# Two graph layers on one core: the second feed-forward products by seven instead of eight in one layer, first products planned first, head products one group at a time, and the layer norm's aggregation on GpSimd

## The chip, the core and the metric

The kernel runs on one core of a Trainium2 chip. Its engines work side by side: TensorE (PE in the profile; its weight loads are PEld) multiplies matrices, VectorE (DVE), ScalarE (ACT) and GpSimd (POOL) do element-wise work, and SyncE (SP) issues the transfers between device memory and the core's SBUF. Matmul results land in PSUM, in 8 banks of 128 partitions by 512 f32 numbers. The metric is the device time of one execution in microseconds (us).

## The reference

64 graphs of 256 nodes and 256 features go through two layers; everything is f32. The inputs are `x` (64, 256, 256) and a 0/1 matrix `adj` (64, 256, 256).

Layer 0 applies graph attention twice and a feed-forward:

```python
Wh = h @ W;  e = leaky_relu(Wh @ a[:F] + (Wh @ a[F:]).T, 0.2)
att = softmax(where(adj > 0, e, -9e15), axis=1);  h = att @ Wh          # twice
h = layernorm(x + h);  h = layernorm(h + relu(h @ w_ff1 + b_ff1) @ w_ff2 + b_ff2)
```

Layer 1 is attention with 8 heads of 32 whose weights are not masked before the softmax; afterwards the values of relation r are summed over the entries where `adj == r` (only 0 and 1 occur), and a feed-forward follows:

```python
attn = softmax(q @ k.T / sqrt(32));  out = sum_r (attn * (adj == r)) @ (src @ Wv[r])
x = layernorm(src + out @ Wo);  x = layernorm(x + gelu(x @ W1 + b1) @ W2 + b2)
```

Both feed-forwards are 256 to 1024 to 256.

## The kernel before, in words

**Tiling.** Two graphs form a pair; 32 pairs go one after another through `whole_way`: `gat_layers`, `feed_forward` (stage 0), `attention`, `feed_forward` (stage 2), and the output's transfer. Activations lie as 4 tiles of 128 nodes by 256 features.

**First feed-forward products (line 689) and query, key and value products (764, 769).** They use a scheme with seven products of matrix halves instead of eight (Strassen's, in Winograd's form). Class `Blocks` holds its steps, named by product: `p1`, `p2`, `p6`, `p5`, `p7`, `p4`, `p3`. Each is two matmuls of 256 columns. The sums of the weights are made once, those of the activations in `Second`. Some products add into a bank that still holds a predecessor: `p6` goes into the bank of `p1` once ScalarE has copied that (line 695), and `p7` into the bank of `p6`, again after a copy. A feed-forward has two such sets of slabs, `a` and `b`, interleaved in one list of steps. ScalarE then applies bias and function (line 701), 16 activations per feed-forward.

**Second feed-forward products (line 720).** By the plain way: for each of two groups of rows `b` and halves `j`, eight matmuls of 256 columns are summed in one bank, 32 in all. `add_rows` (571) adds the bank to the rows, and `layernorm` follows: VectorE's statistics and aggregation (581, 582), GpSimd's root in four small operations (587 to 590), ScalarE's normalisation (594).

**Attention.** Four head groups per pair (two graphs by two sets of four heads). `scores` (809) runs four 32-row matmuls side by side, ScalarE takes the exponentials (818), VectorE masks (822) and half-sums (826) them. `products` (840, 843) runs four 32-column matmuls side by side and sums the weights by a matmul with ones; VectorE takes the reciprocal of a whole 128x256 block (852) and multiplies (853); ScalarE checks the range (850). The head products of two groups are planned together.

**What sets the order.** Nothing loops over pairs at run time: a planner, `run`, writes one fixed order per engine while the program is built. Every piece of VectorE, ScalarE, GpSimd and SP work is given to `put` with an assumed duration, a rank and the events that it waits for; TensorE's work is written as generators that `yield` the events and the number of banks that their next step needs. `run` keeps a clock per engine, always takes the engine that can begin first, and on it the piece of lowest rank. On TensorE it picks among up to four pairs, plus `reliefs` (work on the weights at the start):

```python
g = going[min(sure, key=lambda n: (going[n][0] is besides, "ff" in (going[n][2] or ()) or alone.get("ff") is going[n][0], n))
```

So a pair in its feed-forward comes after all pairs that are elsewhere; only one pair at a time may be in a feed-forward (`alone["ff"]`), and one in attention. `hurried` names the stages in which rows are transposed on TensorE (line 655) instead of through device memory.

## Time and profile before

| | |
|---|---|
| median of 3 runs | 3081.23 us (3080.15 to 3081.99) |
| profiled execution, its own time | 3077.64 us |
| its span, first to last instruction | 3075.9 us |
| mean granted TensorE clock | 0.994 |
| TensorE busy | 3010.9 us, 19154 matmul records |
| TensorE weight loads busy | 2454.7 us |
| VectorE busy | 2234.0 us |
| ScalarE busy | 1835.1 us |
| GpSimd busy | 1032.2 us |

An f32 matmul appears as two records, each with its weight load. Records of consecutive matmuls overlap, so their mean duration (380 ns at 256 columns) is longer than the distance from one start to the next. A line number is that of the program text; several layers share a line, and tile names tell them apart (`w_L_gnn_w_ff` is layer 0, `w_L_gnn_W` layer 1).

### The profile page before, as it was taken

To read this page: it belongs to the slowest core of one execution; us is meant where nothing else is said; L and a number is where in the kernel's file an instruction comes from. 1 tells how busy PE (TensorE), PEld (TensorE's weight loads), DVE (VectorE), ACT (ScalarE), POOL (GpSimd) and SP (SyncE) were. 2 spreads that over 40 slices of the span, in tenths; PEclk is the share of its full clock that TensorE was granted. 3 is DMA by queue.
4 is the path that set the end of the run, shared out by engine and by line. 5 is a ranking of instruction groups with operands and counts; after the bars stand their busy time and mean duration, and the time that the engine had idled before them with its cause. 6 is when DMAs were issued, how large, how long until landed. Compare 5 with 4: busy or idle time off the path is not lost.

```text
span 3075.9 us, 52423 instructions
## 1 busy us (share of the span) xinstructions
PE 3010.9 (98%) x19154; PEld 2454.7 (80%) x19154; DVE 2234.0 (73%) x4411; ACT 1835.1 (60%) x4186; POOL 1032.2 (34%) x1542
## 2 busy tenths in 40 slices
PE   7999999999999999999999999999999999999998
PEld 6877778877878788887888778878788778788876
DVE  5787766788776867768677676686776777767774
ACT  4556665656665566565756566565666565655654
POOL 1332244232423243232352322533325333233223
PEclk8999999999999999999999999999999999999999
DMA  6211132102321122211231122311213211121000
GB/s 181 73 51 36 56 124 79 46 28 75 109 66 50 61 76 80 73 49 56 76 99 60 42 70 69 97 66 50 66 54 96 82 53 57 62 93 58 32 1 22
DMA packets 211865, 205.76 MB, mean 67 GB/s; under 512 B 22928, under 2 KB 171280, under 8 KB 211600
## 3 DMA queue, kind: packets, MB, share of 16 engines
q1 hardware_dynamic: 211184, 202.06, 20.5%
q8 instruction: 154, 2.52, 0.3%
q14 instruction: 111, 0.91, 0.1%
q10 hardware_dynamic: 416, 0.26, 0.0%
HBM read 137.51 MB, written 64.73 MB: 66 GB/s over the span
## 4 chain that ended last, share of the span: by engine, by line
PE 79%; DVE 10%; ACT 3%; DMA 3%; POOL 2%; issue 2%; SPq 1%; DVEq 0%; POOLq 0%; ACTq 0%
PE ps L720 24%; PE ps L689 20%; PE ps L840 6%; PE ps L764 6%; PE ps L769 6%; PE ps L809 4%; PE ps L545 3%; PE ps L529 3%; PE ps L862 2%; PE ps L843 2%; DVE e L502 2%; DVE x L571 2%; DVE st L581 1%; PE ps L558 1%; DMA home<-yb 1%
## 5 line engine op out<-in xcount | busy, mean ns | idle before, releaser
L587 POOL TENSOR_SCALAR less<-mv 128x2 f32<-128x2 f32 x256 | 65.4, 255 | 1596.6 <-DVE mv L582 1561.4
L594 ACT ACTIVATE x<-x,less,rstd 128x256 f32<-128x256 f32 x512 | 279.3, 594 | 418.8 <-POOL less L590 414.9
L720 PE MATMUL ps<-w_L_gnn_w_ff,ff 128*128 128x256 f32 x2048 | 466.4, 380 | 0.0
L720 PE MATMUL ps<-w_L_gnn_W,ff 128*128 128x256 f32 x2048 | 461.7, 380 | 0.9 <-ACT ff L701 0.9
L720 PEld LDWEIGHTS ps<-w_L_gnn_W,ff 128*128 128x128 f32 x2048 | 386.9, 190 | 61.0 <-issue 5.4
L720 PEld LDWEIGHTS ps<-w_L_gnn_w_ff,ff 128*128 128x128 f32 x2048 | 387.9, 190 | 57.2 <-issue 4.3
L393 DVE TENSOR_TENSOR ff<-ps,ff 128x512 f32<-128x512 f32 x384 | 261.1, 683 | 163.6 <-PE ps L689 127.1
L822 DVE TENSOR_TENSOR m<-a,adj 128x1024 f32<-128x1024 f32 x256 | 325.4, 1271 | 20.6 <-ACT a L818 20.5
L689 PE MATMUL ps<-yT,w_L_gnn_W1p 128*128 128x256 f32 x1280 | 316.1, 384 | 10.9 <-ACT ff L695 7.4
L689 PE MATMUL ps<-yT,w_L_gnn_w_ff1p 128*128 128x256 f32 x1280 | 312.4, 384 | 12.3 <-ACT ff L695 12.3
L818 ACT ACTIVATE a<-ps 128x512 f32<-128x512 f32 x512 | 266.8, 603 | 68.0 <-PE ps L809 67.1
L689 PEld LDWEIGHTS ps<-yT,w_L_gnn_W1p 128*128 128x128 f32 x1280 | 238.3, 190 | 61.8 <-ACT ff L695 17.9
L689 PEld LDWEIGHTS ps<-yT,w_L_gnn_w_ff1p 128*128 128x128 f32 x1280 | 241.3, 191 | 56.6 <-ACT ff L695 16.7
L571 DVE TENSOR_TENSOR x<-ps,x 128x512 f32<-128x512 f32 x256 | 173.0, 680 | 152.4 <-PE ps L720 120.3
L695 ACT ACTIVATE ff<-ps 128x512 f32<-128x512 f32 x384 | 221.1, 589 | 92.0 <-PE ps L689 90.1
L604 POOL TENSOR_TENSOR x<-x,b_L_gnn_g_ln 128x512 f32<-128x512 f32 x128 | 168.7, 1318 | 274.5 <-DVE yb L623 138.3
L852 DVE RECIPROCAL h<-ps 128x256 f32<-128x256 f32 x128 | 224.1, 1752 | 49.1 <-PE ps L843 48.9
L581 DVE BATCH_NORM_STATS2 st<-x 128x6 f32<-128x256 f32 x512 | 208.4, 407 | 4.7 <-issue 0.4
L701 ACT ACTIVATE ff<-ff,c_L_gnn_b_ff 128x256 f32<-128x256 f32 x384 | 174.4, 509 | 49.4 <-DVE ff L393 48.8
L604 POOL TENSOR_TENSOR x<-x,b_L_gnn_g 128x512 f32<-128x512 f32 x128 | 166.1, 1298 | 94.4 <-ACT x L594 74.8
L589 POOL TENSOR_TENSOR rstd<-rstd,mhalf 128x2 f32<-128x2 f32 x256 | 189.1, 739 | 21.3
L701 ACT ACTIVATE ff<-ff,c_L_gnn_b 128x256 f32<-128x256 f32 x384 | 172.0, 502 | 31.6 <-DVE ff L393 31.0
(138 smaller groups left out, 5499.8 us busy)
## 6 DMA issues: line engine op xcount, KB each, us to landing
home<-yb SPq DMA_DIRECT2D x182, 256.0 KB, 2.0
yT<-home SPq DMA_DIRECT2D x728, 64.0 KB, 2.0
rows<-row SPq DMA_DIRECT2D x60, 512.0 KB, 3.8
input<-in_xT SPq DMA_DIRECT2D x32, 512.0 KB, 4.0
x<-in_x SPq DMA_DIRECT2D x32, 512.0 KB, 4.1
out<-x SPq DMA_DIRECT2D x32, 512.0 KB, 2.9
input<-in_adjT SPq DMA_DIRECT2D x30, 512.0 KB, 4.1
v<-in_adjT SPq DMA_DIRECT2D x2, 512.0 KB, 6.6
```

What stands on the lines that cost most here:

```text
L393: nc.vector.tensor_tensor(self.target(c, h), self.bank[bank], self.target(c, h), ALU.add)
L571: return put("vector", 0.6, lambda: nc.vector.tensor_tensor(rows, p, rows, ALU.add), *events, frees=["bank"])
L581: nc.vector.bn_stats(st[:, j, :], rows[j])
L594: nc.scalar.activation(rows[j], rows[j], AF.Identity, bias=less[:, j:j + 1], scale=rstd[:, j:j + 1])
L604: nc.gpsimd.tensor_tensor(both, both, v.rearrange("p (k d) -> p k d", k=1).to_broadcast([P, 2, D]), op)
L689: nc.tensor.matmul(to, lhsT=w1[:, a, (t + slab) * P:(t + slab + 1) * P], rhs=b, **flags)
L695: return put("scalar", 0.5, lambda: nc.scalar.activation(target(c, h), blocks.bank["x"], AF.Copy), event, rank=-1)
L701: evacuated[h][m] = put("scalar", 0.4, lambda m=m, to=to, source=source: nc.scalar.activation(to, source, func, bias=b1[:, m:m + 1]), even ...
L720: nc.tensor.matmul(p2[:, j * D:(j + 1) * D], lhsT=f[m][:, (2 * j + b) * P:(2 * j + b + 1) * P], rhs=w2[:, m, :], start=m == 0, stop=m == N ...
L818: nc.scalar.activation(a[n][q][:, k], ps[2 * q + k], AF.Exp)
L822: nc.vector.tensor_tensor(m[n][q], a[n][q], adj, ALU.mult)
L852: there = put("vector", 1.68, lambda: nc.vector.reciprocal(s, po[:, N:]), there, rank=0)
```

## The change

- `SEVEN = (0,)`: the second feed-forward products of stage 0 (layer 0) are made by `by_seven`, with seven products of halves of 4 x 2 matmuls of 128 columns each. `last_weights` loads that weight in four parts and `last_sums` makes four differences of them. VectorE makes four combinations of the activations in place (`combine`, 128x1024) and adds the products to the rows as they come (`add`). Stage 2 keeps the plain way (`by_eight`). The activations now lie in four tiles, one for each quarter.
- `degree`: first feed-forward products come before other pairs' work, second ones after it. `filling` marks the pair whose second products are under way. Five pairs may be in flight instead of four.
- Head products are planned for one head group at a time, and the order of a few steps in attention moves.
- The reciprocal works on 8 numbers per partition between two transposes of 32x32 blocks; the range check works on those.
- The layer norm's aggregation of two half-row statistics moves from VectorE to GpSimd, whose root has nine operations.
- `put_each` gives exponentials, normalisations, statistics and scalings to the planner one instruction at a time, ranked by when the first was ready.

```diff
...
+SEVEN = (0,)
...
+    def put_each(engine, us, emits, *events, rank=1, frees=(), needs=None, function=None):
+        before = None
+        for emit in emits[:-1]:
+            before = put(engine, us, emit, *events, rank=rank, lag=0.0, needs=needs, function=function, behind=before)
+            events, needs = [before], None
+        return put(engine, us, emits[-1], *events, rank=rank, frees=frees, function=function, behind=before)
...
+        def degree(g):
+            if g[0] in filling:
+                return 2
+            return 0 if "ff" in (g[2] or ()) or alone.get("ff") is g[0] else 1
...
-                g = going[min(sure, key=lambda n: (going[n][0] is besides, "ff" in (going[n][2] or ()) or alone.get("ff") is going[n][0], n))
+                g = going[min(sure, key=lambda n: (going[n][0] is besides, degree(going[n]), n))
-                piece = waiting[engine].pop(min(able, key=lambda n: (waiting[engine][n]["rank"], waiting[engine][n]["ready"])))
+                piece = waiting[engine].pop(min(able, key=lambda n: (waiting[engine][n]["rank"], waiting[engine][n]["first"]["ready"])))
...
+    def last_weights(name):
+        s = const.tile([P, 7, NF // 2, P], F32, name="w_" + name)
+        for c, h, at in ((1, 0, 0), (0, 0, 1), (0, 1, 2), (1, 1, 3)):
+            nc.sync.dma_start(s[:, at], t[name][c * FF // 2:(c + 1) * FF // 2, h * P:(h + 1) * P].rearrange("(k p) d -> p k d", p=P))
+        return s
+    def last_sums(w, there, event):
+        for to, a, b in ((4, 3, 0), (5, 2, 4), (6, 2, 3), (3, 1, 5)):
+            there = put("vector", 0.6, lambda to=to, a=a, b=b: nc.vector.tensor_tensor(w[:, to], w[:, a], w[:, b], ALU.subtract),
+                        there, rank=5, event=event if to == 3 else None)
...
-        st = mv = rstd = less = None
+        st = rstd = less = None
         rows = [r[:, 2 * b + j, :] for j in range(2)]
-        def statistics():
-            nonlocal st, mv
-            st, mv = small.tile([P, 2, 6], F32, name="st"), small.tile([P, 2, 2], F32, name="mv")
-            for j in range(2):
-                nc.vector.bn_stats(st[:, j, :], rows[j])
-                nc.vector.bn_aggr(mv[:, j, :], st[:, j, :])
+        def statistics(j):
+            nonlocal st
+            if j == 0:
+                st = small.tile([P, 2, 6], F32, name="st")
+            nc.vector.bn_stats(st[:, j, :], rows[j])
         def root():
             nonlocal rstd, less
-            rstd, less = small.tile([P, 2], F32, name="rstd"), small.tile([P, 2], F32, name="less")
-            nc.gpsimd.tensor_scalar(less, mv[:, :, 0], -1.0, None, ALU.mult)
-            nc.gpsimd.tensor_scalar(rstd, mv[:, :, 1], EPS, None, ALU.add)
+            rstd, less, both, apart = (small.tile([P, 2] if n < 2 or n == 3 else [P, 2, 2], F32, name=name)
+                                       for n, name in enumerate(("rstd", "less", "both", "apart")))
+            halves = [st[:, :, 3 * n + 1:3 * n + 3] for n in range(2)]
+            nc.gpsimd.tensor_tensor(apart, halves[0][:, :, 0], halves[1][:, :, 0], ALU.subtract)
+            nc.gpsimd.tensor_tensor(both, *halves, ALU.add)
+            nc.gpsimd.tensor_tensor(apart, apart, apart, ALU.mult)
+            nc.gpsimd.tensor_scalar(rstd, both[:, :, 1], 1.0 / D, EPS, ALU.mult, ALU.add)
+            nc.gpsimd.tensor_scalar(apart, apart, 0.25, None, ALU.mult)
+            nc.gpsimd.tensor_scalar(less, both[:, :, 0], -0.5, None, ALU.mult)
+            nc.gpsimd.tensor_tensor(rstd, rstd, apart, ALU.add)
             nc.gpsimd.tensor_tensor(rstd, rstd, mhalf[:, :2], ALU.pow)
             nc.gpsimd.tensor_tensor(less, less, rstd, ALU.mult)
-        def normalise():
-            for j in range(2):
-                nc.scalar.activation(rows[j], rows[j], AF.Identity, bias=less[:, j:j + 1], scale=rstd[:, j:j + 1])
-        there = put("vector", 0.9, statistics, *events)
-        there = put("gpsimd", 1.5, root, there, rank=0)
-        return put("scalar", 0.8, normalise, there)
+        def normalise(j):
+            nc.scalar.activation(rows[j], rows[j], AF.Identity, bias=less[:, j:j + 1], scale=rstd[:, j:j + 1])
+        there = put_each("vector", 0.35, [lambda j=j: statistics(j) for j in range(2)], *events)
+        there = put("gpsimd", 2.7, root, there, rank=0)
+        return put_each("scalar", 0.5, [lambda j=j: normalise(j) for j in range(2)], there)
...
+        yield from (by_seven if stage in SEVEN else by_eight)(y, normal, f, evacuated, w2, w2_there, b)
+        for g in range(2):
+            normal[g] = layernorm(y, g, *normal["added"][g])
+            if onwards:
+                transposed(y, normal[g], normal, g, pair, 1)
+            else:
+                normal[g] = scaled(y, ln[3], g, normal[g])
+        filling.clear()
+        done_with("ff")
+    def by_eight(y, normal, f, evacuated, w2, w2_there, last):
+        half, order, normal["added"] = NF // 2, (0, 1, 4, 5, 2, 3, 6, 7), []
+        filling.append(alone["ff"])
...
-                        nc.tensor.matmul(p2[:, j * D:(j + 1) * D], lhsT=f[m][:, (2 * j + b) * P:(2 * j + b + 1) * P],
+                        nc.tensor.matmul(p2[:, j * D:(j + 1) * D], lhsT=f[c][j][:, k, g * P:(g + 1) * P],
                                          rhs=w2[:, m, :], start=m == 0, stop=m == NF - 1)
...
+            normal["added"].append([add_rows(y, p2, g, there, normal["scaled", g])])
+    def by_seven(y, normal, f, evacuated, w2, w2_there, last):
...
+        half = NF // 2
+        (a22, a12), (a21, a11) = f
+        def done(j, c):
+            return evacuated[j][c * half:(c + 1) * half]
+        def product(n, to, side, first=False):
+            for b in range(2):
+                for k in range(half):
+                    nc.tensor.matmul(to[:, b], lhsT=side[:, k, b * P:(b + 1) * P], rhs=w2[:, n - 1, k],
+                                     start=first and b == k == 0, stop=True, skip_group_check=True)
+            return took(1.8)
+        def add(to, of, us, *events, frees=()):
+            return put("vector", us, lambda: nc.vector.tensor_tensor(to, of, to, ALU.add), *events,
+                       *(normal["scaled", b] for b in range(2)), rank=-1, frees=frees)
+        def combine(to, a, b, op, *events):
+            return put("vector", 1.14, lambda: nc.vector.tensor_tensor(to, a, b, op), *events, rank=0)
+        def two_halves():
+            return bank().rearrange("p (j b d) -> p j b d", j=2, b=2)
+        rows = y.rearrange("p (b j) d -> p j b d", j=2)
+        def quarter(j, h):
+            return rows[:, 1 - j, :, h * P:(h + 1) * P]
+        yield [w2_there, *done(0, 0)], None, 1
+        left = two_halves()
+        read4 = product(4, left[:, 0], a22, True)
+        t1 = combine(a22, a21, a22, ALU.add, *done(0, 0), *done(0, 1), read4)
+        t3 = combine(a21, a11, a21, ALU.subtract, *done(1, 1), t1)
+        yield done(1, 1), None, 1
+        x = two_halves()[:, 0]
+        read1 = product(1, x, a11, True)
+        d1 = add(quarter(0, 0), x, 0.34, read1)
+        t2 = combine(a11, a22, a11, ALU.subtract, t3, read1)
+        yield from last.p3()
+        frees_at(clock["tensor"], ["yT", "sums_yT"])
+        filling.append(alone["ff"])
+        yield [t1], None, 1
+        v = two_halves()[:, 0]
+        read5 = product(5, v, a22, True)
+        d5 = add(quarter(1, 1), v, 0.34, read5)
+        yield [t2, d1], None, 0
+        d6 = add(quarter(0, 1), x, 0.34, product(6, x, a11))
+        yield done(1, 0), None, 0
+        read2 = product(2, left[:, 1], a12)
+        d24 = add(rows[:, :, :, :P], left, 0.6, read2, read4, frees=["bank"])
+        t4 = combine(a12, a12, a11, ALU.subtract, t2, read2)
+        yield [t3, d6], None, 0
+        d7 = add(rows[:, 0].rearrange("p b (h d) -> p b h d", h=2),
+                 x.rearrange("p b (h d) -> p b h d", h=1).to_broadcast([P, 2, 2, P]), 0.6, product(7, x, a21), d5, frees=["bank"])
+        yield [t4, d5], None, 0
+        d3 = add(quarter(0, 1), v, 0.34, product(3, v, a12), frees=["bank"])
+        normal["added"] = [[d24, d7, d3]] * 2
...
-            def weight(q):
-                a[n][q] = work.tile([P, 2, 512], F32, name="a", bufs=HQ)
-                for k in range(2):
-                    nc.scalar.activation(a[n][q][:, k], ps[2 * q + k], AF.Exp)
+            def weight(q, k):
+                if k == 0:
+                    a[n][q] = work.tile([P, 2, 512], F32, name="a", bufs=HQ)
+                nc.scalar.activation(a[n][q][:, k], ps[2 * q + k], AF.Exp)
...
+            blocks = s.rearrange("p (g i) -> p g i", i=32)
+            both = []
+            def invert():
+                both.append(small.tile([P, 2, N // 32], F32, name="inverse", bufs=4))
+                nc.vector.transpose(s, po[:, N:])
+                nc.vector.tensor_copy(both[0][:, 1], blocks[:, :, 0])
+                nc.vector.reciprocal(both[0][:, 0], both[0][:, 1])
+                nc.vector.transpose(blocks, both[0][:, 0].rearrange("p (g i) -> p g i", i=1).to_broadcast([P, N // 32, 32]))
             def check():
-                for of, c in ((s, 0), (po[:, N:], 1)):
-                    nc.scalar.activation(of, of, AF.Copy, accum_out=reach[:, pair, c, n:n + 1])
-            there = put("vector", 1.68, lambda: nc.vector.reciprocal(s, po[:, N:]), there, rank=0)
-            there = put("vector", 0.34, lambda: nc.vector.tensor_tensor(to, po[:, :N], s, ALU.mult), there, rank=0)
-            put("scalar", 1.0, check, there, frees=["bank", "h"])
-            return there
+                for of in range(2):
+                    nc.scalar.activation(both[0][:, of], both[0][:, of], AF.Copy, accum_out=reach[:, pair, of, n:n + 1])
+            there = put("vector", 1.3, invert, there, rank=0)
+            put("scalar", 0.4, check, there, rank=3)
+            return put("vector", 0.34, lambda: nc.vector.tensor_tensor(to, po[:, :N], s, ALU.mult), there, rank=0, frees=["bank", "h"])
...
-        for step in (a_.p1, b_.p1, a_.p2, a_.p6, b_.p2, a_.p5, b_.p6, a_.p7, b_.p5, a_.p4, b_.p7, lambda: scores(0), a_.p3, b_.p4,  b_.p3, lambda: scores(1)):
+        for step in (a_.p1, b_.p1, a_.p2, a_.p6, b_.p2, a_.p5, b_.p6, a_.p7, b_.p5, a_.p4, b_.p7, a_.p3, b_.p4, lambda: scores(0), b_.p3, lambda: scores(1)):
...
-        for n in (0, 2):
-            yield [*masked[n], *masked[n + 1], ready["v", 0, n // 2], ready["v", 1, n // 2]], None, 2
-            divided += [products(n), products(n + 1)]
-            if n == 0:
-                for later in (2, 3):
-                    yield from scores(later)
+        for n in range(4):
+            yield [*masked[n], ready["v", 0, n // 2], ready["v", 1, n // 2]], None, 1
+            divided.append(products(n))
+            if n < 2:
+                yield from scores(n + 2)
...
-    run(reliefs(), (whole_way(pair) for pair in range(NPAIR)), 4)
+    run(reliefs(), (whole_way(pair) for pair in range(NPAIR)), 5)
...
-    nc = bacc.Bacc("TRN2", target_bir_lowering=False, num_devices=1)
+    nc = bacc.Bacc("TRN2", target_bir_lowering=False, num_devices=1, dynamic_dma_scratch_size=1024)
```

## The prediction

> **What bounds the kernel now.** I read the busy table of the page first, then the groups by shape, TensorE in order of time, the start of the trace, and last TensorE's waits.
>
> ```profile
> PE 3010.9 (98%) x19154; PEld 2454.7 (80%) x19154; DVE 2234.0 (73%) x4411; ACT 1835.1 (60%) x4186; POOL 1032.2 (34%) x1542
> ```
>
> TensorE bounds it. Its busy time hides waits, since overlapping records run 0.38 us each, so I count from start to start.
>
> ```profile
> 1002.24 8.90 PE L720 MATMUL ps<-w_L_gnn_W,ff 128*128 128x256 f32 x40
> 1011.07 1.07 PE L840 MATMUL ps<-a,v 128*32 128x256 f32 x16
> 1011.96 1.05 PE L840 MATMUL ps<-m,v 128*32 128x256 f32 x16
> 1012.82 0.61 PE L843 MATMUL ps<-h,ones 128*32 128x256 f32 x8
> 1013.25 1.05 PE L840 MATMUL ps<-a,v 128*32 128x256 f32 x16
> 1014.12 1.05 PE L840 MATMUL ps<-m,v 128*32 128x256 f32 x16
> 1014.98 0.61 PE L843 MATMUL ps<-h,ones 128*32 128x256 f32 x8
> 1015.53 1.78 PE L862 MATMUL ps<-w_L_gnn_Wo,qk 128*128 128x256 f32 x7
> ```
>
> An f32 matmul leaves two records. Forty records of 256 columns last (8.90 - 0.38)/39 = 0.218 us each, 0.216 in the median: 0.432 us per matmul. The column-tiled head products (L840, L843) stand in blocks of two head groups, 4.46 us for both.
>
> If every record took its own pace (0.216 us at 256 columns, a quarter of that where four run side by side), TensorE would need 2902.6 us. The span is 3075.9: 6.8 us before the first matmul, 12.7 after the last began, and 153.8 beyond the pace. Of these about 54 are entering and leaving the 32-wide blocks (0.31 us for each of 128 score blocks, 0.23 for each of 64 product blocks), 23 are waits of the first 100 us, and 72 are waits between full-width matmuls later.
>
> ```profile
> PE ps L689 <- ACT ff L695: 23.5, 31, 1.7
> PE ps L558 <- ACT xw L510: 11.6, 2, 10.6
> PEld ps L689 <- ACT ff L695: 44.3, 55, 2.1
> ```
>
> Columns: who waited for whom, total us, times, longest. Of the 72 us, 51 are the first feed-forward products (L689) waiting for ScalarE's copy of their own predecessor's bank (L695). Going through the seven-product scheme step by step, 29 of the 51 stand at one step, the seventh product of the second half (p7 of slabs b), and 7 at p6 of slabs a.
>
> [...]
>
> The halved products need 128 columns per freshly loaded weight, which the feed-forward never does here. The start of the trace brackets it:
>
> ```profile
> 51.75 1.86 PEld L933 LDWEIGHTS ps<-c_L_gnn_b_ln2c,wqk 128*128 128x128 f32 x16
> 50.99 1.04 PE L465 MATMUL ps<-ident,rise 128*128 128x128 f32 x8
> 51.86 1.84 PE L933 MATMUL ps<-c_L_gnn_b_ln2c,wqk 128*128 128x1 f32 x16
> ```
>
> Full f32 loads before one-column matmuls: (1.86 - 0.19)/15 = 0.112 us each, which is what the load alone allows[...]. 128-column transposes: (1.04 - 0.27)/7 = 0.109 us, which is what the columns alone allow. At 256 columns the load (0.19 us as recorded) vanishes under the matmul. Overlapped, the pace is the larger, 0.112 us per record, 0.2234 per matmul; in series it would be 0.22 per record. I take 0.112 and keep 0.109 and 0.22 as ends.
>
> **The change, part by part.** Counts are from the two built programs.
>
> *Seven products in the first layer's second half.* 1024 matmuls of 256 columns go (1024 x 0.4317 = 442.1 us), 1792 of 128 come (1792 x 0.2234 = 400.4). On TensorE: **-41.7 us**, all of it on the path. What it adds lies on VectorE: 128 combinations of 128x1024 at L822's mean of 1.27 us (+163) and 128 additions of 256 columns from PSUM at 0.41, the mean of the like-sized L853 (+53); 64 additions of 0.68 replace 64. New waits: product 5 on the first combination, 6 on the third, 3 on the fourth. The built order leaves 4.7 us of other matmuls or more before 5 and 4.4 before 6, but in 14 of 32 stages product 3 follows 2 with only product 7 (1.79 us) between; addition and combination need 0.68 + 1.27 plus handovers, 2.2 or 2.3. 14 x 0.5: **+7 us** (0 if nothing else holds VectorE up and the handovers are short, +25 if its queue adds a microsecond each).
>
> *First products first, second ones last, five pairs at once.* TensorE's work is the same; distances change. p7 of slabs b stands at the bare minimum of two products (1.73 us) behind its predecessor in 53 of 64 feed-forwards before, 17 after; p6 of slabs a in 54 and 64. Scaling the measured losses: 29 x (1 - 17/53) = 20 won, 7 x 10/54 = 1 lost, about **-18 us** after rounding down. From below, nothing is won if ScalarE, which must fit six copies and sixteen activations into one first half, is simply late elsewhere; from above, nearly all 72 go. The end loses cover: before, 24 records and more of another pair's second products stood between the last pair's projections and its feed-forward; after, the last output projection is followed directly by 32 transposes and then the first products. A layer norm costs, by its rows, 0.69 + 0.8 + 2.5 + 1.1 us and handovers, then a copy of 0.6 and one sum of 0.5, minus the transposes: **+8 us**.
>
> *Products per head group.* Runs of head products: 64 before, 120 after, 8 of them still double. A split costs 0.093 (entry) + 0.113 (leaving instead of running on) + 0.025 = 0.231 us: 56 x 0.231 = +12.9. Scores next to products 64 times instead of 8 save an entry of 0.093 each: -5.2. **+7.7 us.** The score-to-product distance shrinks to 6.9-7.2 us at the least (8.3 before); the masks and half sums were done 6.1 to 6.9 us after the scores in the median, up to 10.7, and are needed only 0.9 and 1.8 us into the block. I take no wait; 0.3 us at each would be +35.
>
> *Aggregation on GpSimd.* VectorE loses 512 aggregations (-93 us); GpSimd's root goes from four operations (0.255 + 0.235 + 0.739 + 0.206) to nine, five more at 0.2 or so: +1.06 us x 256 = 271, to 43%. Behind it on GpSimd stand the scalings and shifts (L604), which have 275 us of slack before them. The layer norm becomes 0.7 us longer; other pairs' matmuls hide that except at the two ends.
>
> *Reciprocal by transposes; split ScalarE pieces; table loads.* VectorE: 1.752 us become two transposes of 256 columns (0.44 by interpolation between L475 and L623), a copy and a short reciprocal, 1.25 together: -64. VectorE in sum 2234 + 163 + 53 - 93 - 64 = 2293, 76%. ScalarE: +48 table loads of 1.28 (+62), checks about -50. None on TensorE's path while both stay under 80%; if that cover fails, it shows as waits of L731, priced above.
>
> *Start.* The weights of the second half come by four transfers instead of one and get four sums of 0.69 us, ahead of the second pair's attention weights on VectorE. Two more microseconds of transfers ahead of the bias that TensorE already waits 10.6 us for: **+2**. SP's later issues in the steady state are the same.
>
> Sum: -41.7 + 7 - 18 + 8 + 7.7 + 2 = **-35 us**. Profiled: span 3075.9 to 3041; the profiled execution was 3077.6, 3.6 below the median of 3081.2. Median: **3046 us**.
>
> **Rivals.**
> *The filler works better.* With second products always ready as filler most of the 72 us go, say 60 instead of 18: 3004 us. For it: the ScalarE pieces are finer, and additions rank by the first piece's time. Against: at most one feed-forward runs at a time, so it has no second products to fill its own first half.
> *Gains eaten.* Score-to-product waits and VectorE's longer queue give back 30 us: 3076, no difference. The change then does nothing that can be told (0.2%, 6 us, is about what this kernel's runs resolve).
> *Slower: the narrow products don't reach their pace.* Place: L804. Price: 3584 records, so each nanosecond is 3.6 us. It decides from 35/3584 = 10 ns more, 0.122 us per record; at 0.13 the time is 3111, wholly in series over 3400. For it: load and columns differ by only 3 ns, so any handover shows. Against: loads start 2 ns after the matmul before them in the trace at 256 columns. A VectorE chain late by more than 1.1 us in every pair would end on the same side.
>
> **How the numbers follow.** Forecast 0.60 (its own range 3025 to 3068), better filler 0.14, gains eaten 0.11, slower 0.15. Range 2998 to 3090: it leaves out about 0.05 below and 0.13 above. Faster: 0.60 + 0.14 + a third of the eaten case = 0.78; same 0.07; slower 0.15.
>
> **What would show it.** L804's records 0.112 us apart; TensorE records up by 1536; waits of L731 on L737 near 50 us instead of 68 (both TensorE queues together); head-product runs near 120; an idle TensorE of some 8 us after the last L990; VectorE near 2290, GpSimd near 1300. The prediction is wrong if L804's pace is over 0.12, if waits for VectorE's combinations (L813) exceed 25 us, or if head products (L960) wait for masks.

## The result, and the profile after

The changed kernel takes 3087.67 us (median of 14 runs, 3079.35 to 3095.08) against 3080.14 for the kernel before on the same chips (14 runs, 3075.55 to 3084.40): a ratio of 1.0024, 95% interval 1.0015 to 1.0034. The forecast was 3046 us. The kernel as built became slightly slower, and the forecast had the wrong sign.

The page of the changed kernel, its busy table (engine, busy us, share of the span of 3086.1 us, instructions):

```profile
PE 2986.8 (97%) x20690; PEld 2474.5 (80%) x20690; DVE 2338.3 (76%) x4543; ACT 1831.8 (59%) x4234; POOL 1345.9 (44%) x2822
```

TensorE has 1536 records more, as counted. Its busy share fell from 98% to 97%: it has less to do and waits longer. Its work in order of time (start, duration, line, count), two runs of the narrow products:

```profile
2019.63 3.73 PE L804 MATMUL ps<-w_L_gnn_w_ff,ff 128*128 128x128 f32 x32
2026.20 1.95 PE L804 MATMUL ps<-w_L_gnn_w_ff,ff 128*128 128x128 f32 x16
```

One record lasts 0.277 us in the mean, so the first line gives (3.73 - 0.28)/31 = 0.111 us from start to start, the second (1.95 - 0.28)/15 = 0.111. The pace of 0.112, the forecast's main number, is right, and so is TensorE's gain: summed over all records at their own pace, 2902.5 us became 2860.8, **-41.7 us**. But what TensorE loses beyond that pace rose from 153.8 to 205.6 us. Its waits after the change (who waited for whom, total us, times, longest):

```profile
PE ps L990 <- DVE qk L983: 13.8, 8, 3.3
PE ps L731 <- DVE ff L424: 11.8, 6, 2.8
...
PE ps L731 <- ACT ff L737: 9.2, 10, 1.5
PE ps L804 <- DVE ff L813: 9.0, 6, 2.4
PE ps L701 <- ACT x L640: 7.7, 3, 3.5
...
PE ps L960 <- DVE m L942: 1.8, 2, 1.1
```

Before, the first line was the wait for ScalarE's copies, and the whole of what named VectorE (DVE) was this:

```profile
PE ps L689 <- DVE x L571: 1.0, 1, 1.0
PE ps L689 <- DVE ff L393: 0.7, 1, 0.7
```

Now the first lines are waits for VectorE: adding all lines of this view that name it gives 38.7 us, against 1.7 before. The wait for ScalarE that the forecast wanted smaller did get smaller (23.5 to 9.2).

One such wait can be followed from its cause. VectorE of the changed kernel in order of time; the bracket is idle time before the instruction and what ended it:

```profile
1524.14 0.48 DVE L542 SCALAR_TENSOR_TENSOR e<-rows,ratio 128x256 f32<-128x256 f32 x1 [1.03 <-DMA rows<-row]
1524.66 1.55 DVE L544 SCALAR_TENSOR_TENSOR e<-adj,empty,e 128x256 f32<-128x256 uint8 x1
...
1526.15 1.48 DVE L542 SCALAR_TENSOR_TENSOR e<-rows,ratio 128x256 f32<-128x256 f32 x1
1527.67 1.37 DVE L544 SCALAR_TENSOR_TENSOR e<-adj,empty,e 128x256 f32<-128x256 uint8 x1
...
1528.97 0.68 DVE L424 TENSOR_TENSOR ff<-ps,ff 128x512 f32<-128x512 f32 x1
...
1531.10 0.43 DVE L972 STREAM_TRANSPOSE h<-ps 128x256 f32<-128x256 f32 x1
...
1532.85 1.38 DVE L544 SCALAR_TENSOR_TENSOR e<-adj,empty,e 128x256 f32<-128x256 uint8 x1
...
1534.35 0.40 DVE L983 TENSOR_TENSOR qk<-ps,h 128x256 f32<-128x256 f32 x1
```

GpSimd (POOL) in the same stretch:

```profile
1524.65 1.29 POOL L650 TENSOR_TENSOR x<-x,b_L_gnn_g_ln 128x512 f32<-128x512 f32 x1
1525.89 1.47 POOL L650 TENSOR_TENSOR x<-x,b_L_gnn_g 128x512 f32<-128x512 f32 x1
1527.31 1.44 POOL L650 TENSOR_TENSOR x<-x,b_L_gnn_b_ln 128x512 f32<-128x512 f32 x1
1528.72 1.45 POOL L650 TENSOR_TENSOR x<-x,b_L_gnn_beta 128x512 f32<-128x512 f32 x1
1532.69 1.26 POOL L650 TENSOR_TENSOR x<-x,b_L_gnn_g 128x512 f32<-128x512 f32 x1 [2.52 <-ACT x L640]
```

And TensorE:

```profile
1526.21 0.61 PE L963 MATMUL ps<-h,ones 128*32 128x256 f32 x8
...
1532.10 0.59 PE L990 MATMUL ps<-w_L_gnn_Wo,qk 128*128 128x256 f32 x2
1534.81 1.56 PE L990 MATMUL ps<-w_L_gnn_Wo,qk 128*128 128x256 f32 x6 [2.12 <-DVE qk L983]
```

L542 lasts 0.48 us in the median, L544 0.49. Beside GpSimd's scalings (L650, 1.26 to 1.47 us here) four of them last about as long as one of those: 1.55, 1.48, 1.37 and 1.38. L424, which reads PSUM and SBUF, runs beside L650 in its ordinary 0.68. The head products end at 1526.8; their inversion (the reciprocal by transposes, from L972 on) begins at 1531.1, behind the stretched operations, its multiplication (L983) at 1534.35, behind one more, and TensorE stands still for 2.12 us.

### The profile page after: what moved, and what is told of

The parts are those of the page before. It is cut to its first block, busy times and chain, and to the rows that moved or that the text cites. A ratio compares the mean times of both kernels' runs of the same rounds, so it can differ in the third digit from the quotient of the medians.

```text
span 3086.1 us, 56707 instructions
## 1 busy us (share of the span) xinstructions
PE 2986.8 (97%) x20690; PEld 2474.5 (80%) x20690; DVE 2338.3 (76%) x4543; ACT 1831.8 (59%) x4234; POOL 1345.9 (44%) x2822
## 5 line engine op out<-in xcount | busy, mean ns | idle before, releaser
L629 POOL TENSOR_TENSOR apart<-st 128x2 f32<-128x2 f32 x256 | 55.0, 215 | 1283.4 <-DVE st L622 1281.3
L778 PE MATMUL ps<-w_L_gnn_W,ff 128*128 128x256 f32 x2048 | 475.0, 382 | 3.6 <-ACT ff L743 3.6
L804 PEld LDWEIGHTS ps<-w_L_gnn_w_ff,ff 128*128 128x128 f32 x3584 | 420.2, 192 | 29.0 <-DVE ff L813 12.7
L804 PE MATMUL ps<-w_L_gnn_w_ff,ff 128*128 128x128 f32 x3584 | 429.9, 277 | 10.0 <-DVE ff L813 9.0
L424 DVE TENSOR_TENSOR ff<-ps,ff 128x512 f32<-128x512 f32 x384 | 262.5, 684 | 158.7 <-PE ps L731 97.9
L640 ACT ACTIVATE x<-x,less,rstd 128x256 f32<-128x256 f32 x512 | 285.5, 594 | 115.7 <-POOL less L637 114.5
L942 DVE TENSOR_TENSOR m<-a,adj 128x1024 f32<-128x1024 f32 x256 | 314.0, 1227 | 49.1 <-ACT a L938 49.1
L737 ACT ACTIVATE ff<-ps 128x512 f32<-128x512 f32 x384 | 225.7, 589 | 161.5 <-PE ps L731 159.7
L731 PE MATMUL ps<-yT,w_L_gnn_W1p 128*128 128x256 f32 x1280 | 316.3, 386 | 1.7 <-ACT ff L737 1.0
L731 PE MATMUL ps<-yT,w_L_gnn_w_ff1p 128*128 128x256 f32 x1280 | 307.8, 382 | 0.0
L731 PEld LDWEIGHTS ps<-yT,w_L_gnn_W1p 128*128 128x128 f32 x1280 | 241.5, 192 | 48.1 <-issue 9.5
L731 PEld LDWEIGHTS ps<-yT,w_L_gnn_w_ff1p 128*128 128x128 f32 x1280 | 241.3, 192 | 31.4 <-ACT ff L737 0.2
L650 POOL TENSOR_TENSOR x<-x,b_L_gnn_g 128x512 f32<-128x512 f32 x128 | 181.6, 1421 | 186.9 <-ACT x L640 165.2
L650 POOL TENSOR_TENSOR x<-x,b_L_gnn_g_ln 128x512 f32<-128x512 f32 x128 | 180.9, 1416 | 168.8 <-DVE yb L669 130.4
L551 ACT ACTIVATE xw<-xw,rs 128x258 f32<-128x258 f32 (+1 forms) x256 | 117.7, 505 | 164.5 <-DVE rs L547 164.0
L813 DVE TENSOR_TENSOR ff<-ff 128x1024 f32<-128x1024 f32 x128 | 182.2, 1423 | 34.5 <-PE ps L804 31.6
L542 DVE SCALAR_TENSOR_TENSOR e<-rows,ratio 128x256 f32<-128x256 f32 x256 | 141.9, 554 | 82.5 <-DMA rows<-row 40.9
```

What stands on the lines that cost most here:

```text
L424: nc.vector.tensor_tensor(self.target(c, h), self.bank[bank], self.target(c, h), ALU.add)
L640: nc.scalar.activation(rows[j], rows[j], AF.Identity, bias=less[:, j:j + 1], scale=rstd[:, j:j + 1])
L650: nc.gpsimd.tensor_tensor(both, both, v.rearrange("p (k d) -> p k d", k=1).to_broadcast([P, 2, D]), op)
L731: nc.tensor.matmul(to, lhsT=w1[:, a, (t + slab) * P:(t + slab + 1) * P], rhs=b, **flags)
L737: return put("scalar", 0.5, lambda: nc.scalar.activation(target(c, h), blocks.bank["x"], AF.Copy), event, rank=-1)
L778: nc.tensor.matmul(p2[:, j * D:(j + 1) * D], lhsT=f[c][j][:, k, g * P:(g + 1) * P], rhs=w2[:, m, :], start=m == 0, stop=m == NF - 1)
```

## The experiments

All are variants of the changed kernel (or of the one before, where said), some of which leave work out; each was timed beside the kernel before, whose median stood between 3078.1 and 3080.1 us in all sets. "Waits for VectorE" is the sum of TensorE's waits that name VectorE, in the profiled execution. "Margin" is the planner's `SLACK` (0.30 elsewhere), the time by which a step of TensorE must have been ready before the planner ranks it.

| kernel | us | ratio to before, 95% | waits for VectorE, us |
|---|---|---|---|
| before | 3080.1 | 1 | 1.7 |
| before, margin 0.34 / 0.25 | 3096.2 / 3077.2 | 1.0040 to 1.0073 / 0.9987 to 1.0001 | 13.0 / 2.3 |
| changed | 3087.7 | 1.0015 to 1.0034 | 38.7 |
| changed, margin 0.32 | 3050.2 | 0.9883 to 0.9914 | 15.4 |
| changed, margin 0.34 | 3077.2 | 0.9979 to 1.0000 | 34.2 |
| changed, margin 0.36 | 3104.9 | 1.0062 to 1.0096 | 58.9 |
| aggregation back, same order | 3066.0 | 0.9938 to 0.9965 | 32.8 |
| the same at margin 0.32 / 0.36 | 3065.6 / 3098.7 | 0.9942 to 0.9969 / 1.0052 to 1.0082 | 31.9 / 52.0 |
| small combinations | 3053.2 | 0.9907 to 0.9937 | 24.5 |
| narrow scalings | 3017.0 | 0.9782 to 0.9812 | 2.9 |
| narrow scalings, margin 0.36 | 3018.7 | 0.9790 to 0.9820 | 7.1 |
| narrow scalings, before | 3053.7 | 0.9908 to 0.9935 | none |

**One part undone.** Four kernels first. The aggregation back on VectorE, the planner's costs unchanged and so every engine's order kept:

```diff
...
             nc.vector.bn_stats(st[:, j, :], rows[j])
+            nc.vector.bn_aggr(mv[:, j, :], st[:, j, :])
...
-            nc.gpsimd.tensor_tensor(apart, halves[0][:, :, 0], halves[1][:, :, 0], ALU.subtract)
-            nc.gpsimd.tensor_tensor(both, *halves, ALU.add)
...
+            nc.gpsimd.tensor_scalar(less, mv[:, :, 0], -1.0, None, ALU.mult)
+            nc.gpsimd.tensor_scalar(rstd, mv[:, :, 1], EPS, None, ALU.add)
...
```

> The changed kernel with one part undone: the layer norm's aggregation is back on VectorE (GpSimd's root has four operations again), and the planner's costs stay as they are, so that every engine's work stands in the order of the changed kernel. [...]taking them away shortens GpSimd by some 270 us, the time that VectorE's operations take beyond the medians of their groups falls from 164 us towards 110, and the waits of the second layer's output projection for the head products' inversion (L983) and of the first feed-forward products for VectorE fall with it: 3070 us or less, although VectorE gets 93 us of aggregations more. Rival, that VectorE is late because of how much it has to do in this order: the 93 us lengthen the same chains, 3092 to 3105 us. If neither matters, 3087.

Measured: 3066.0 us, 21.6 less, within the first range; but not for the reason given with it. The time of VectorE's operations beyond the medians of their groups (operations that lasted over 60 ns longer than the median of their line, tile and shape, summed) did not fall: 164 us, and 168 with the aggregation back. So GpSimd's short operations, as far as this run shows, do not stretch VectorE's. What did fall are the waits behind the root: ScalarE's for GpSimd's result from 114.5 to 48.8 us.

The other three are planned anew: `SEVEN = ()`, the old rule of precedence, and head products in twos.

```diff
-SEVEN = (0,)
+SEVEN = ()
```

> The changed kernel with the seven products undone: the first layer's second feed-forward products are the eight plain ones of 256 columns, everything else as changed. Theory that the seven products keep most of their 41.7 us and that the loss is elsewhere: 3087 + 42 - 18 (the waits for their combinations) = 3110 us. Theory that VectorE's 216 us of combinations and additions make it late for everything else and so give the gain back: 3087 or less, with VectorE's busy time near 2125 us, the output projection's wait for the inversion (L983) down from 13.8 + 19.5 us to under 12 in both queues, and the half-clock windows back from 12 to about 6.

Measured: 3131.0 us (1.0149 to 1.0177), 43 more than changed. TensorE's loss beyond its pace is the same as with the seven products (207.4 and 205.6 us), so between these two plans they keep their 41.7 us. The clock that the kernel's planner keeps says the same: it ends for TensorE at 2967 us in the changed kernel and at 3013 without the seven products. The theory that they give their gain back finds no support here.

```diff
-            if g[0] in filling:
-                return 2
-            return 0 if "ff" in (g[2] or ()) or alone.get("ff") is g[0] else 1
+            return "ff" in (g[2] or ()) or alone.get("ff") is g[0]
```

> The changed kernel with the old rule of precedence: a feed-forward's products all come after other work that is ready, instead of first products first and second ones last. Order theory: the new rule puts VectorE's results too close ahead of the products that read them; with the old one the output projection's wait for the inversion falls from 23.1 us towards 3.4 and TensorE's waits at full-width products from 104 to about 85: 3068 us, while the first feed-forward products wait for ScalarE's copies some 12 us more. Against it, that the new rule wins what was forecast (17 of 29 us at p7): 3100 us.

```diff
-        for n in range(4):
-            yield [*masked[n], ready["v", 0, n // 2], ready["v", 1, n // 2]], None, 1
-            divided.append(products(n))
+        for n in (0, 2):
+            yield [*masked[n], *masked[n + 1], ready["v", 0, n // 2], ready["v", 1, n // 2]], None, 2
+            divided += [products(n), products(n + 1)]
...
```

> The changed kernel with the head products planned two groups at a time, as before. Runs of head products fall from 120 to 64: the entries and exits alone are worth 7.7 us, 3080. Order theory: the split also brings scores and products closer and puts each inversion behind other VectorE work; then the class of 32-wide blocks falls from 78 to 60 us and the output projection's waits fall as well: 3065. If the plan merely shuffles, 3087 plus or minus 8.

Measured: 3144.1 (1.0190 to 1.0218) and 3160.8 us (1.0247 to 1.0275), both far above either theory. The order theory finds no support: in these plans the old rule and the twos make the kernel slower. The loss is in the planned order already: the planner's clock ends for TensorE at 3061 and 3056 us in these two, against 2967.

**What on GpSimd costs.** Five idle operations of two columns in the root of the kernel with the aggregation back, behind the four or ahead of them:

```diff
...
             nc.gpsimd.tensor_tensor(less, less, rstd, ALU.mult)
+            for n in range(5):
+                nc.gpsimd.tensor_tensor(idle[:, 0], less, rstd, ALU.mult)
...
```

> The kernel with the aggregation back on VectorE (3066 us), and five idle GpSimd operations of two columns (0.2 to 0.25 us each, two inputs from SBUF, results unused) behind each layer norm's root, nothing else. [...]lie outside the chain from statistics to normalisation. If the 21.6 us that the aggregation cost come from GpSimd's load[...], most of them return: 3080 to 3090 us. If they come from the length of the chain itself, 3066 plus at most 4.

> As the kernel with five idle operations behind the root, but with the five ahead of the root's four, so that the chain from the statistics to the normalisation is longer by 1.1 to 1.2 us, and VectorE still does the aggregation. Chain theory: ScalarE's normalisation waits longer with the copies and activations of other pairs queued behind it; the 21.6 us return, and more of them than with the operations behind: 3085 to 3100 us. Load theory: the same as with the operations behind. If neither load nor chain is the cause[...], 3066.

Measured: 3119.7 (1.0104 to 1.0135) and 3158.6 us (1.0237 to 1.0265), 54 and 93 above 3066. Both theories of cost were right in direction, and both sizes are larger than expected. These short operations add next to nothing to VectorE's stretch (172 and 152 us beyond the medians, 168 without them), so what they cost comes through queues. Behind the root they delay the scalings, and SyncE's output transfers wait for those, with the loads that VectorE needs behind them in SyncE's order:

```profile
SPq L1110 <- POOL x L647: 113.1, 30, 12.8
```

That is SyncE's view with the operations behind; without them it is 64.7 us (18 times). VectorE's waits for the transfers of `rows` and `home` went from 61.9 to 127.9 us. Ahead of the root, ScalarE's waits for it rise from 48.8 to 266.7 us.

**The seven products alone**: old precedence, twos, four pairs in flight, aggregation on VectorE.

```diff
...
-    run(reliefs(), (whole_way(pair) for pair in range(NPAIR)), 5)
+    run(reliefs(), (whole_way(pair) for pair in range(NPAIR)), 4)
```

> The changed kernel with everything undone that can be but the seven products: the old rule of precedence, head products planned two groups at a time, four pairs in flight, aggregation on VectorE (finer ScalarE pieces and the inversion by transposes stay). If the seven products are sound by themselves and the losses are the other parts': the kernel before less 41.7 us plus some 10 to 15 of waits for combinations, 3050 us. If the seven products need the new order (their combinations come late where second products aren't kept as filler), waits at L804 exceed 40 us and the time is 3090 or more.

Measured: 3086.6 us (1.0016 to 1.0029), between the two. TensorE loses 40.0 us at L804's products (forecast: 7) and 49.2 us wait for VectorE: in this plan, without the new order, the seven products give back what they win.

**What a reshuffle is worth.** A null change, to tell the change from its plan:

```diff
-SLACK = 0.3
+SLACK = 0.32
```

> A null change: the changed kernel with the planner's margin 0.32 instead of 0.30 us, which reshuffles the plan without a reason of its own. It measures what a reshuffle alone is worth. If plans of this kind are alike, 3087 plus or minus 8 us; if the plan of the changed kernel is a lucky or an unlucky draw, 25 us or more away, and then the runs that undo a part and are planned anew (44 to 73 us slower) can't be read part by part.

> A second null change to the changed kernel: the planner's margin 0.34 us instead of 0.30, which gives another order on every engine with the same work. Theory that the change is worth what was forecast and that its own plan is a bad draw: 3030 to 3070 us, as the margin 0.32 gave 3050. Theory that 0.32 was the lucky draw and the change is worth nothing: 3075 to 3110.

> A third null change to the changed kernel, margin 0.36 us. The same two theories: 3030 to 3070, or 3075 to 3110. If the four plans of the changed kernel scatter over more than 50 us with no centre, then no single plan of a part undone can be read to better than that.

> A null change to the kernel before: margin 0.34 us instead of 0.30, which gives it another order on every engine. If the kernel before has a lucky plan among its own, 3090 to 3130 us; if its plans are alike (it has fewer products that come just in time), 3080 plus or minus 8.

> A second null change to the kernel before, margin 0.25 us. As for the margin 0.34: 3090 to 3130 if its own plan is a lucky draw, 3080 plus or minus 8 if its plans are alike. The forecast compared one plan with one plan; the comparison of the two groups of plans is what the forecast's sum of -35 us is really about.

The same work in four orders takes 3050, 3077, 3088 and 3105 us; the kernel before in three, 3077, 3080 and 3096. Means of 3080 and 3084.5: as groups the two can't be told apart. The first null run is the second case of its expectation, a plan 37 us away from another of the same work, and so the 43 to 73 us of the three kernels planned anew can be read only roughly; the next two runs fall on the side on which 0.32 is the good draw. The kernel before gave one plan of each kind, 3096 and 3077. The scatter has an order, though: in the four plans of the changed kernel the time rises with TensorE's waits for VectorE (15, 34, 39, 59 us). The planner's clock has them in the same order but closer together: it ends at 2951, 2956, 2967 and 2969 us, 18 us apart in place of 55. The rest is something that the planner does not know. At margin 0.32 the changed kernel is faster than the kernel before (0.9899).

The aggregation moved back inside two of these orders:

> The plan of the margin 0.32 (3050 us) with the aggregation back on VectorE and every engine's order kept. If the 21.6 us that the move of the aggregation cost are general: 3028 to 3035 us. If they belong to the one plan, where VectorE and GpSimd happened to be late together: 3045 to 3055, or slower, since VectorE gets 93 us more.

> The same step in the plan of the margin 0.36 (3105 us), where TensorE waits longest for VectorE (59 us). General cost: 3080 to 3088 us. One plan's affair: 3100 to 3115, and if VectorE's own work is what makes it late, above 3115.

15.4 us slower (3065.6) and 6.2 faster (3098.7, between the two ranges), after 21.6 faster in the first order: the aggregation's cost belongs to the plan, and its mean can't be told from nothing.

**What makes VectorE late.** Two kernels in the changed kernel's order, one with less work for VectorE, one with less for GpSimd:

```diff
-            return put("vector", 1.14, lambda: nc.vector.tensor_tensor(to, a, b, op), *events, rank=0)
+            return put("vector", 1.14, lambda: nc.vector.tensor_tensor(to[:, :1], a[:, :1], b[:, :1], op), *events, rank=0)
```

> The changed kernel in its own order, with each of the 128 combinations made on a quarter of its columns (one slab of four; the rest of the seven products' operands is left uncombined), which takes some 0.95 us from each and 120 us from VectorE. Theory that VectorE's own work makes it late: waits of TensorE for VectorE fall from 39 us to under 20, also those of the output projection and the first products that have nothing to do with the combinations, and the time falls to 3040 to 3055 us. Theory that GpSimd beside it makes it late: only the waits for the combinations themselves (9 us) go: 3070 to 3080.

```diff
-            nc.gpsimd.tensor_tensor(both, both, v.rearrange("p (k d) -> p k d", k=1).to_broadcast([P, 2, D]), op)
+            nc.gpsimd.tensor_tensor(both[:, :, :32], both[:, :, :32], v[:, :32].rearrange("p (k d) -> p k d", k=1).to_broadcast([P, 2, 32]), op)
```

> The changed kernel in its own order, with GpSimd's 512 scalings and shifts (L650) made on 32 of 256 columns (the others are left unscaled), which takes some 1.1 us from each and 580 us from GpSimd. VectorE's work stays. Theory that GpSimd beside VectorE makes it late: VectorE's time beyond the medians of its groups falls from 164 us to under 80, TensorE's waits for VectorE fall to under 20 us, 3040 to 3060 us. Theory that VectorE's own work does it: 3080 to 3087.

Small combinations: 3053.2 us, 34.4 less for 87.6 us less of busy VectorE (2338.3 to 2250.7; 120 were expected). Beside the combinations' own readers (9.0 to 1.1 us) the first products gain (L731's wait for L424, 11.8 to 6.3), the output projection does not (13.8 to 16.2), and all waits for VectorE fall to 24.5 us, not under 20. The time lies in the range of the theory of VectorE's own work, the waits do not: that work is a part of the cause.

Narrow scalings: 3017.0 us, 70.6 less, more than the theory of GpSimd beside VectorE asked for. VectorE's time beyond the medians falls from 164 to 5 us. It has the same instructions and spends 161.6 us less on them (engine, busy us):

```profile
PE 2970.7 (98%) x20690; PEld 2474.8 (82%) x20690; DVE 2176.7 (72%) x4543; ACT 1833.0 (61%) x4234; POOL 806.7 (27%) x2822
```

Where the 161.6 us were is read from VectorE's groups by shape (count, then busy us, mean ns of one). The changed kernel:

```profile
L424 DVE TENSOR_TENSOR ff<-ps,ff 128x512 f32<-128x512 f32 x384 | 262.5, 684 | 158.7 <-PE ps L731 97.9 <-ACT ff L737 47.6 <-ACT ff L743 10.3
L622 DVE BATCH_NORM_STATS2 st<-x 128x6 f32<-128x256 f32 x512 | 190.6, 411 | 6.5
...
L813 DVE TENSOR_TENSOR ff<-ff 128x1024 f32<-128x1024 f32 x128 | 182.2, 1423 | 34.5 <-PE ps L804 31.6 <-ACT ff L743 1.3
L544 DVE SCALAR_TENSOR_TENSOR e<-adj,empty,e 128x256 f32<-128x256 uint8 x256 | 147.9, 578 | 9.1
...
L973 DVE COPY inverse<-h 128x8 f32<-128x8 f32 x128 | 32.3, 252 | 4.4
```

With narrow scalings:

```profile
L424 DVE TENSOR_TENSOR ff<-ps,ff 128x512 f32<-128x512 f32 x384 | 263.1, 685 | 181.2 <-PE ps L731 107.6 <-ACT ff L737 55.2 <-ACT ff L743 15.5
L622 DVE BATCH_NORM_STATS2 st<-x 128x6 f32<-128x256 f32 x512 | 190.9, 413 | 6.5
...
L813 DVE TENSOR_TENSOR ff<-ff 128x1024 f32<-128x1024 f32 x128 | 155.6, 1216 | 34.1 <-PE ps L804 32.5
...
L544 DVE SCALAR_TENSOR_TENSOR e<-adj,empty,e 128x256 f32<-128x256 uint8 x256 | 125.2, 489 | 9.1
...
L973 DVE COPY inverse<-h 128x8 f32<-128x8 f32 x128 | 22.1, 172 | 4.4
```

The combinations fall from 1423 to 1216 ns, L544 from 578 to 489, the inversion's small copy from 252 to 172. The additions that read PSUM (L424, 684 and 685 ns) and the statistics with one input (L622, 411 and 413) do not move. What sets the two kinds apart is not shown. Of TensorE's waits for VectorE, these are left:

```profile
PE ps L990 <- DVE qk L983: 1.5, 1, 1.5
...
PE ps L960 <- DVE m L942: 0.8, 1, 0.8
```

(and two of 0.6 us together). Narrow scalings also shorten GpSimd's queue: ScalarE's waits for the root fall from 114.5 to 71.2 us, SyncE's for the scalings from 70.0 to 32.7. With the idle operations, work on GpSimd alone cost 54 and 93 us, and no run separates it here from the stretch.

The trace allows an estimate. Let every instruction of the changed kernel's trace start again as soon as the one ahead of it on its engine and everything that it waits for are through, each with the delay that it had, and replace durations alone. With VectorE's and GpSimd's durations out of the kernel with narrow scalings, the end comes 55 us earlier, or 70 where the slow products behind a wait (last section) become fewer with that wait; the two measured spans differ by 69.3. With VectorE's durations alone it comes 42 or 52 us earlier, with GpSimd's alone 10 or 11. In the plan of margin 0.36, which follows, both give 64 or 85 (measured 86.2), VectorE's alone just as much, GpSimd's alone 1 or 2. For the kernel before it falls short: 17 or 19 of 25.8. By this estimate the stretch of VectorE's operations is about three quarters of the effect or more, and GpSimd's queue the small part. It is worked out from the traces and not measured.

The scalings stand in the kernel before as well, so the last two kernels ask what they cost there, and in the slowest plan:

> The kernel before, in its own order, with GpSimd's 512 scalings and shifts made on 32 of 256 columns (the others are left unscaled), as was done to the changed kernel. [...]the kernel before, in which TensorE waits only 2 us for VectorE, gains little, 3060 to 3079 us, although VectorE's time beyond its medians falls from 94 us to under 15; and the two kernels without the scalings then stand 43 us or more apart, the forecast's sum and more. If the scalings cost both kernels alike (some 70 us): 3005 to 3015, and the change is still worth nothing.

> The changed kernel with the margin 0.36 (3105 us, the slowest of its plans), and GpSimd's scalings narrowed in the same way, order kept. If the scatter of the plans is how often each lets GpSimd's scalings meet VectorE's chains: within 20 us of the other plan without them (3017), so 3010 to 3040 us. If the plan itself is worse: 3060 us or more.

The kernel before gains 24.4 us, 3053.7, for 86.9 us less of VectorE time (2234.0 to 2147.1):

```profile
PE 3001.0 (98%) x19154; PEld 2453.1 (80%) x19154; DVE 2147.1 (70%) x4411; ACT 1838.5 (60%) x4186; POOL 542.7 (18%) x1542
```

VectorE's time beyond the medians falls from 94 to 3 us, as expected; the gain is somewhat more than expected. The slowest plan falls by 86.2 us, to 3018.7, within 2 us of the other. Its TensorE waits, at margin 0.36 with full scalings:

```profile
PE ps L731 <- DVE ff L424: 27.9, 10, 4.2
PE ps L884 <- DVE qk L424: 14.3, 11, 2.6
```

and with narrow ones:

```profile
PE ps L731 <- DVE ff L424: 3.3, 6, 0.9
```

Two plans 17 us apart (3088 and 3105) are 2 us apart without the scalings, as in the planner's clock (2967 and 2969). And the change, judged without them, is worth what was forecast: 3018.7 against 3053.7, timed in the same set, a ratio of 0.9885, about 0.9865 to 0.9905 with the half widths of the two intervals added in squares, or **-35 us**; in the changed kernel's own order -36.7. That is less than the 43 us or more of the first case in the expectation for the kernel before, since that kernel gained too. It rests on two plans of the changed kernel and one of the kernel before.

## Why the prediction was wrong

The forecast's sum against TensorE's clock, in us. The middle column is the change as it is, from the spans 3075.9 and 3086.1; the last the same change between the two kernels with narrow scalings, 3050.1 and 3016.8.

| term | forecast | measured | without the scalings |
|---|---|---|---|
| TensorE's own pace | -41.7 | -41.7 | -41.7 |
| waits between full-width products (+7 and -18) | -11 | +32.1 | -16.0 |
| 32-wide blocks, transposes, tail (+7.7 and +8) | +15.7 | +19.2 | +18.1 |
| first 100 us, start, end | +2 | +0.5 | +6.2 |
| sum | -35 | +10.1 | -33.4 |

(The spans themselves differ by +10.2 and -33.3.) Three lines of four hold with the scalings; without them all four do within 5 us. That the sum then meets the forecast so closely is luck in part, since the second line gained more than forecast and the third and fourth lost more. The failure is one line, 43 us in size. The prediction's three signs of being wrong did not show it: the pace was 0.111, the waits for L813 9.0 us (21.7 in both queues), those of L960 for masks 1.8.

*Seven products.* The pace was right to 1 ns. Their waits, +7, were 17.9 us at L804, and 8.9 without the scalings. Nearly all stand where they were forecast, at product 3, in 14 of 32 stages. The price was right for combinations of 1.27 us (1.22 without the scalings), while those of the changed kernel took 1.42 in the mean and up to 2.31.

*First products first, second ones last.* Forecast 51 us of waits down to 33; measured 36.8, and without the scalings 34.1 down to 9.1. What changed is who is late: TensorE's wait for ScalarE's copies (L737, both TensorE queues) is 23.9 us instead of 68, below the 50 expected, and VectorE's additions (L424) fill the place with 26.3. The step foresaw only ScalarE being late elsewhere.

*Products per head group.* The text looked for waits ahead of the head products, took none, and was right: L960 waits 1.8 us for masks. The wait came behind them. The output projection (L990) lost 3.5 us before and loses 23.1 after, because the inversion waits its turn on VectorE. No step priced it. Without the scalings it is 5.0.

*The tail* came nearly as forecast (+8): after the last output projection TensorE idles 6.4 us for its transposes. The changed kernel, TensorE in order of time:

```profile
3033.13 1.89 PE L990 MATMUL ps<-w_L_gnn_Wo,qk 128*128 128x256 f32 x8
3037.89 1.35 PE L701 MATMUL ps<-ident,x 128*32 128x128 f32 x32 [2.87 <-ACT x L640]
3042.76 2.00 PE L701 MATMUL ps<-ident,x 128*32 128x128 f32 x32 [3.51 <-ACT x L640]
```

*VectorE and ScalarE in sum.* This is the step that failed: "None on TensorE's path while both stay under 80%; if that cover fails, it shows as waits of L731, priced above." VectorE stayed at 76% (2338 us, 45 more than in the forecast) and was on the path all the same, and the longest of these waits stands at L990, not at L731. The 80% was the author's estimate; no trace shows such a limit. Each engine runs its queue in a fixed order, so a microsecond lost anywhere ahead of an inversion, an addition or a combination can arrive there. The forecast put it at nothing. Measured, a microsecond of VectorE time was worth 34.4/87.6 = 0.39 us of the kernel (combinations) and 70.6/161.6 = 0.44 (scalings, with what GpSimd's shorter queue gives), in the kernel before 24.4/86.9 = 0.28. These are no general price: with the aggregation back VectorE is busy 78.1 us longer (2416.4), and the kernel is 21.6 us faster, as the waits for the root are shorter.

The stretch itself was in the trace of the kernel before: its mask multiply (L822) takes 1.22 us in the median and up to 2.30 (min, median, max in ns):

```profile
L822 DVE TENSOR_TENSOR m<-a,adj x256: 1164/1220/2303, 154.9 to 3005.4; 128x1024 f32<-128x1024 f32 x128
```

Nothing of it was carried into the sum. What the scalings cost VectorE rose from 86.9 to 161.6 us. Its time beyond the medians rose by 70 us (94 to 164): 36 of them at the combinations (26) and the inversion's copy (10), new operations that narrow scalings shorten (1423 to 1216 ns and 252 to 172 in the mean), the rest at operations that both kernels have and that lose more in the new order. The cost to the kernel rose from 24.4 to 70.6 us. The difference, 46 us by the medians and 43.5 by the profiled spans, is what separates the two measured columns above.

The rival "gains eaten" had the right mechanism (VectorE's longer queue) at 30 us instead of 43; the sentence on a VectorE chain late in every pair ended on the right side. What remains open: how the 70.6 us divide between stretch and queue is estimated and not measured, and other plans of the two kernels could shift the comparison of groups.

## What to carry to other kernels

A busy share does not tell whether an engine is off the path: here VectorE was on it at 76%. Price added work on an engine with a fixed queue by what stands behind it, and count what its operations lose to a neighbour, which the trace shows as operations far above their group's median (here 164 us in sum). Where a planner sets the order, run the same work in several orders before reading one kernel against another: here the order alone was worth 55 us, more than the change. Remove a disturbance on both sides of a comparison: only with the scalings narrowed in both kernels did the rest of the forecast's sum show.

## What the runs showed of the hardware

Four runs of L542 and L544 beside GpSimd's scalings of 1.26 to 1.47 us lasted 1.37 to 1.55 us, against medians of 0.48 and 0.49. The inversion's copy of eight columns (L973, median 0.17 us) went up to 1.01. With the scalings narrowed, VectorE's time beyond the medians fell from 164 to 5 us in the changed kernel and from 94 to 3 in the one before. GpSimd's scalings themselves take 1298 to 1323 ns in the means of the groups before and 1400 to 1443 after, with medians of 1272 to 1277 ns in both kernels.

Six waits of the changed kernel were followed by a loss beyond their own length. After one of 2.21 us, the next products run at about half their pace:

```profile
1591.79 1.03 PE L731 MATMUL ps<-sums_yT,w_L_gnn_W1p 128*128 128x256 f32 x4
1595.02 1.73 PE L731 MATMUL ps<-sums_yT,w_L_gnn_W1p 128*128 128x256 f32 x4 [2.21 <-DVE ff L424]
1596.55 1.91 PE L731 MATMUL ps<-yT,w_L_gnn_W1p 128*128 128x256 f32 x4
```

Four records take 1.03 us before it, 1.73 and 1.91 behind it, and the trace has a granted clock of 0.50 from 1595.4 to 1598.8 us. Between 100 and 3000 us nine waits of the changed kernel are 2.0 us or longer. Such a stretch follows six of them, with 1.8 us lost each (3.0 behind the longest, of 3.28 us); it does not follow the other three, of 2.05 to 2.12 us, the one in the section on the result among them, nor any shorter wait. What decides is not shown. The mean granted clock of the changed kernel is 0.989 against 0.994 before.
